# A two-layer convolution megakernel: conv 1's stores on ScalarE's queue, and another order of loads and work where the layers meet

## The chip, the cores and the metric

The program runs on one core of one Trainium2 chip. The metric is device time in microseconds of one execution, from which the median of several runs is taken. The engines are called PE (TensorE's matmuls), PEld (its weight loads), DVE (VectorE), ACT (ScalarE), POOL (GpSimd) and SP (SyncE, which only issues transfers here).

## What is computed

Two residual layers on x of 4 images, 64 channels, 256 x 256, all in float32.

```python
def layer0(v):                                   # v = group_norm(x)
    h = gelu(conv3x3(v, c1_w))
    xa, k = split(conv1x1(h, c2_w))
    xs = gelu(conv_vertical3(conv_horizontal3(xa)))         # depthwise
    mask = top2(softmax(mean(xs) @ gate_w.T))               # per image
    out = xs + sum(mask[i] * w3[i](w2[i](k) * w1[i](xs)) for i in range(3))
    return conv1x1(out, proj_w)

def layer1(v):                                   # v = group_norm(y)
    h = relu(batch_norm(conv3x3(v, quantize(w1)) + b1))     # statistics over all 4 images
    h = batch_norm(conv3x3(h, quantize(w2)) + b2)
    return relu(h + v)

y = x + layer0(group_norm(x))
result = y + layer1(group_norm(y))
```

A group norm needs the whole image before it can be applied, the mask needs an image's whole `xs`, and a batch norm needs all four images. These are what divide the work into passes.

## The kernel before

Tensors lie with 64 channels times two halves of the rows on the 128 partitions. An image is cut into 16 chunks of 8 rows a partition (`NCH`; 1 MB each) and, for layer 0's outputs, into 32 octets of half that size (`NOCT`). There are five stages.

1. **Front**: for each of 64 units (an image's chunk), layer 0's 3x3 convolution, the taps, the gelu and the low-rank terms. Results `xs` and the ranks go to DRAM (`xs_d`, `low_d`).
2. **Layer 0's outputs**: once an image's mask is known, its octets are made: `low_load`, `xs_load` and `out_load` (the residual x, tile `y`) bring the inputs, `out_slot` runs 16 matmuls (`out_open`, tile `ps_o`), adds them to `y` on DVE (`out_add`, L848), takes statistics, and after every second octet `out_store` (L861) sends `y` to `y_d`. Images 0, 1 and most of image 2 are done between the units of the front. The last 10 octets of image 2 and all 32 of image 3 are done between the chunks of stage 3 (`plan_out_late`).
3. **Conv 1** of layer 1: `conv1_load` brings normal rows of `y_d` (tile `yn`, L882), POOL takes row differences (L342), ACT normalises and copies them (L345, L358, L900), DVE makes the lower halves (L352 in `conv1_lower`, L361 in `conv1_lower_odd`), PE runs 12 matmuls on odd rows (`conv1_odd`, tile `ps_hm`) and two groups of 12 (`conv1_even`, tile `ps_h`) a chunk, ACT makes the shared term `m` (L311), DVE makes the result `h` in two halves (`conv1_out`, L317), ACT squares it for the statistics (`conv1_square`, L381), and a store sends it to `h1_d` (L956; the profile leaves numbers out and calls it `h_d`).
4. **Conv 2** over all 64 chunks, from `h1_d`.
5. **The end**: batch norm, residual sums and the store of the result.

**What sets the order.** Every engine works in its program's order. In stages 1 to 3 that order is written out by hand: `at(step, order, call)` puts a call in a table, and the calls are issued sorted by step and, in a step, by order. A unit of the front has two steps, so the front has 128; conv 1 begins at step `CONV1` = 128, and each chunk has four: chunk k of image b has its odd matmuls at T = 128 + 65 b + 4 k. `plan_conv1` puts a chunk's load at T - 13, its differences at T - 7, its result's two halves at T + 8/3 and T + 4, and its square at T + 16/3. For chunks 0 to 2 of image 0 the places are lists of their own. `TAIL` says where the last units' steps fall among conv 1's: `front_taps_h` (L683, L686), `front_taps_i` (L677), `front_k_out` (L733) and others. `divide` is a small POOL instruction (L485) that waits for the taps' matmuls.

All transfers are issued by SP, in the same order: an issue that waits (for a result, a free buffer, or the landing of an earlier transfer) holds up all issues behind it. Completion is told by eight semaphores taken in turn.

**Buffers that matter here.** `y` has two, of 1 MB (tag "o"); the late `xs_in` shares three (tag "h"); `ranks` has two. Conv 1's `h` has two in turn, chosen in `conv1_out`, but for image 0 the chunks 0, 1 and 2 all take the same one:

```python
if k % 2 and (b > 0 or k > 2):
    h_out[b, k] = flat(chunk_x(f"h1_{b}_{k}"))[:, 0 : CPAIR * W].rearrange("p (a b) -> p a b", b=W)
else:
    h_out[b, k] = conv1_pool[0].tile([P, CPAIR, W], F32, tag="h1", name=f"h1_{b}_{k}", bufs=1)
```

Of the kernel before, what the change touches and what calls it, by code (L numbers as in the profile page):

```python
# [27 lines left out]
NG = NPAIR // GP  # L28
NOCT = NG // 2
CG = 4  # L30
CPAIR = CG * GP
# [10 lines left out]
def conv_preact_kernel(ctx: ExitStack, tc: tile.TileContext, io, col128, colset, col64):  # L42
    nc = tc.nc
# [21 lines left out]
    h1_d = [dram.tile([P, NSKEW, W], F32, name=f"h1_d{b}") for b in range(B)]  # L65
    h2_d = [dram.tile([P, NPAIR, W], F32, name=f"h2_d{b}") for b in range(B)]

    def flat(t):
        return t.rearrange("p a b -> p (a b)")
# [23 lines left out]
    def chunk_x(name):  # L93
        return first_pool.tile([P, CPAIR, PW], F32, tag="x", name=name, bufs=1)
# [25 lines left out]
    def at(step, order, call, *args):  # L120
        plan[step, order].append((call, args))
# [9 lines left out]
    def c128(name):  # L131
        return m128[:, col128[name][0] : col128[name][1]]
# [152 lines left out]
    def group_norm(st, avg, out, name):  # L285
        mv = stat.tile([P, 1, 2], F32, tag="mv", name=f"mv_{name}")
        nc.vector.bn_aggr(mv[:, 0, :], flat(st))
        yield
        yield from combine(mv, 1, avg, eps, out, name)
# [89 lines left out]
    def square(name, h, junk, total, rows=slice(0, P)):  # L379
        n = h.shape[1] * W  # L380
        nc.scalar.activation(  # L381
            junk[rows, 0:n], flat(h), AF.Square, bias=less[name][rows], accum_out=total
        )
# [440 lines left out]
    def out_open(b, n):  # L824

        k, sub, i = n // 2, n % 2, n % 4
        if n == 0:
            st_y[b] = lstat.tile([P, NG, 6], F32, tag="st_y", name=f"st_y{b}")
        ps = open_o[b, n] = bank("p", f"ps_o_{b}_{n}")
        xs = xs_in[b, k][:, sub]  # L830
        low = lows[b, k // 2].rearrange("p s (r w) -> p s r w", w=W)
        rounds(
            *(
                [
                    ((ps[:, x], p, x, c128("proj"), xs[:, :, p, :], (0, 2)), dict(start=True, stop=False, skip_group_check=True)),
                    ((ps[:, x], p, x, wm[b][:, i, :], low[:, :, p, :], (0, 2)), dict(start=False, stop=True, skip_group_check=True)),
                ]
                for x in range(2)
                for p in range(2)
            )  # L840
        )
# [4 lines left out]
    def out_add(b, n):  # L846
        ps, y = open_o.pop((b, n)), out_rows(b, n)
        nc.vector.scalar_tensor_tensor(y, ps.rearrange("p x s w -> p x (s w)"), out_bias[b], y, ALU.add, ALU.add)  # L848

    def out_stats(b, n):  # L850
        y = out_rows(b, n)
        for i in range(2):
            nc.vector.bn_stats(st_y[b][:, 2 * n + i, :], y[:, i])
        if n % 2:
            k = n // 2
            del xs_in[b, k]
            if k % 2:
                del lows[b, k // 2]

    def out_store(b, k):  # L860
        nc.sync.dma_start(y_d[b][:, k * CPAIR : (k + 1) * CPAIR, :], ys.pop((b, k)))  # L861

    def out_slot(b, n):
        out_open(b, n)
        out_add(b, n)
        out_stats(b, n)
        if n % 2:
            out_store(b, n // 2)

    def out_end(b):  # L870
        gn2[b] = const.tile([P, 3], F32, name=f"gn2_{b}")
        yield from group_norm(st_y.pop(b), c128("avg4"), gn2[b][:, 0:2], f"y{b}")
        nc.vector.tensor_scalar(gn2[b][:, 2:3], gn2[b][:, 0:1], gn2[b][:, 1:2], -1.0, ALU.mult, ALU.mult)
# [64 lines left out]
    def conv1_out(b, k, g):  # L938
        if g == 0:
# [4 lines that stand above are left out]
        h = h_out[b, k]  # L944
        at_h = h[:, 4 * g : 4 * g + 4, :]
        first = k == g == 0
        total = sums[b][:, 2 * k + g : 2 * k + g + 1]
        leave(at_h, open_h.pop((b, k, g)), m_in[b, k][:, g], "w1", None if first else total)
        if first:
            nc.vector.tensor_reduce(total, h[:, 1:4, :], AX.XY, ALU.add)  # L950
            nc.vector.tensor_reduce(sums[b][0:C, NOCT : NOCT + 1], h[0:C, 0, :], AX.X, ALU.add)
            if b == 0:
                totals_less("h1", h[:, 1:3, :])
        if g:
            del m_in[b, k]
            nc.sync.dma_start(h1_d[b][:, k * CPAIR : (k + 1) * CPAIR, :], h)  # L956

    def conv1_square(b, k):
        h = h_out.pop((b, k))
        square("h1", h[:, 1:, :] if k == 0 else h, junks[0], squares[b][:, k : k + 1])  # L960
        if k == 0:
            square("h1", h[0:C, 0:1, :], junks[0], squares[b][0:C, NCH : NCH + 1], slice(0, C))

    def conv1_end(b):

# [48 lines left out]
    def at_each(places, chain):  # L1014

        for place in places:
            at(*place, next, chain, None)

    F_STEPS = NOCT
    CONV1 = B * F_STEPS  # L1020
# [2 lines left out]
    TAIL = {  # L1023
        (0, 1.15): (0, 1.15), (0, 1.55): (0, 1.55), (0, 4.7): (0, 4.7), (0, 2): (0, 2), (0, 2.2): (0, 2.2),
        (0, 4): (0, 13.2), (0, 4.15): (0, 13.3), (0, 5.2): (0, 13.4), (0, 5.3): (0, 13.5), (0, 8.6): (1, 13.9),
        (0, 9.2): (3, 13.35), (0, 7): (2, 13.2), (0, 7.2): (2, 13.25), (0, 8): (3, 13.1), (0, 9): (3, 13.2), (0, 9.1): (3, 13.3),
        (1, 1.15): (3, 13.4), (1, 1.55): (3, 13.5), (1, 4.7): (4, 13.9), (1, 2): (5, 13.2), (1, 2.2): (5, 13.25),
        (1, 4): (6, 13.2), (1, 4.15): (6, 13.3), (1, 5.2): (6, 13.4), (1, 5.3): (6, 13.5), (1, 8.6): (7, 13.9),
        (1, 8): (8, 13.2), (1, 8.1): (8, 13.3),
# [128 lines left out]
    def plan_out_late(b, ns, steps, order, end):  # L1158

        for n, step in zip(ns, steps):  # L1160
            if n % 2 == 0:
                at(step - 5, 0.2, low_load, b, n // 2)
                at(step - 5, 0.3, xs_load, b, n // 2, "h")
                at(step - 4, 0.4, out_load, b, n // 2)
            at(step, order, out_slot, b, n)
        at_each(end, out_end(b))

    def conv1_first():
# [12 lines left out]
    def plan_conv1(b):  # L1181
        t = CONV1 + b * (NG + 1)
        if b == 0:
            at(t - 4, -1, conv1_first)
            at(t, 12, conv1_open)
        for k in range(NCH):
            T = t + 4 * k
            places = [T + p for p in (-13, -7, -6, -5, -4, -4, -4, -3)]
            if b == 0 and k < 3:
                places = [t + p for p in ((-6, -3, -3, -2, -2, -2, -1, -1), (-4, -1, -1, 0, 0, 0, 0, 1), (-2, 1, 2, 3, 4, 4, 4, 5))[k]]  # L1190
            load, diff, odd, up0, up1, low_odd, low0, low1 = places

            def late(step, order):
                return (step, 5.5 + (order - 13) if step < t else order)

            at(load, 0, conv1_load, b, k)
            at(*late(diff, 13.08), conv1_differences, b, k)
            at(*late(odd, 13.1), conv1_upper_odd, b, k)
            at(*late(up0, 13.12), conv1_upper, b, k, 0)
            at(*late(up1, 13.14), conv1_upper, b, k, 1)  # L1200
            at(*late(low_odd, 13.2), conv1_lower_odd, b, k)
            at(*late(low0, 13.22), conv1_lower, b, k, 0)
            at(*late(low1, 13.24), conv1_lower, b, k, 1)
            at(T, 13, conv1_odd, b, k)
            at(T + 4 / 3, 13, conv1_even, b, k, 0)
            at(T + 4 / 3, 13.15, conv1_shared, b, k)
            at(T + 8 / 3, 13, conv1_even, b, k, 1)
            at(T + 8 / 3, 13.05, conv1_out, b, k, 0)
            at(T + 4, 13.05 if k < NCH - 1 else 12.9, conv1_out, b, k, 1)
            at(T + 4 + 4 / 3, 13.16, conv1_square, b, k)  # L1210
        at(t + NG, 12.95, conv1_end, b)
        at(t + NG + 1, 13.06, conv1_end_out, b)
        at(t + NG + 3, 13.3, conv1_close, b)

    plan_front()
    for b in range(B):
        if b < B - 1:
            plan_stats(b + 1)
            plan_out(b, NOCT if b < B - 2 else 22)
            if b == B - 2:  # L1220
                plan_out_late(b, range(22, NOCT), [CONV1 + 16 + 3 * n for n in range(10)], 13.6, [(CONV1 + n, 12.6) for n in (48, 50, 50, 52, 52, 52, 54)])
        else:
            t, e = CONV1 + 42, CONV1 + b * (NG + 1) - 10
            steps = [t + (e - 6 - t) * n // (NOCT - 1) for n in range(NOCT)]
            plan_out_late(b, range(NOCT), steps, 13.6, [(e - i, 15) for i in (5, 3, 3, 1, 1, 1, -1)])
        plan_conv1(b)
# [116 lines left out]
    with tc.manual_schedule(  # L1343
# [8 lines left out]
        n = len(chunks)  # L1352
# [62 lines left out]
    for i, (b, k) in enumerate(steps):  # L1415
        if i + AHEAD < len(steps):
            end_load(i + AHEAD)
        y, h = y_of.pop(i), h2.pop((b, k))
# [120 lines left out]
```

## Time and profile before

| | |
|---|---|
| median of 3 runs | 3040.98 us (3035.65 to 3042.23) |
| profiled execution | 3027.39 us, span of the program's instructions 3025.4 us |
| PE busy in the span | 2364.3 us (78%) |
| DVE busy | 2467.0 us (82%) |
| ACT busy | 2054.0 us (68%) |
| POOL busy | 1677.4 us (55%) |
| moved by DMA | 915.35 MB, mean 303 GB/s |
| mean granted clock of PE | 0.912 |

The page is one profiled execution. Its engine rows count an engine as busy while an instruction runs, not while it waits; a row of waits gives engine, line and what ended the wait, with microseconds in total, the number of times and the longest. "SPq" is SP's queue, so its rows tell what the issue of transfers stood waiting for. In the chain of waits a "DMA" piece reaches from a transfer's issue to its landing. Conv 1's first matmuls start at 1320 us, its last end at 2025; conv 2 runs from 2035 to 2585.

### The profile page before, as it was taken

How to read it: one execution, taken by the hardware profiler on the slowest of the kernel's cores; microseconds unless marked ns; L12 is line 12 of the kernel's file. 1: busy time of each engine (PE TensorE's matmuls, PEld its weight loads, DVE VectorE, ACT ScalarE, POOL GpSimd, SP SyncE). 2: the span in 40 equal slices, each digit the busy share in tenths (PEclk: the TensorE clock that was granted, in tenths of full speed). 3: DMA queues.
4: the chain of work that ended last, by engine and by line, in shares of the span. 5: the costliest groups of instructions: out<-in, count | busy, mean ns of one | idle time of the engine just before them, and what ended most of it. 6: DMA issues, size and time to landing. Idle time of an engine off the chain costs nothing.

```text
span 3025.4 us, 53036 instructions
## 1 busy us (share of the span) xinstructions
PE 2364.3 (78%) x21576; PEld 1504.4 (50%) x21576; DVE 2467.0 (82%) x2793; ACT 2054.0 (68%) x2274; POOL 1677.4 (55%) x1210
## 2 busy tenths in 40 slices
PE   1898899998999999978889999989999999100000
PEld 1444444444544445545556667767888888100000
DVE  5668688888888899968788888979998998876665
ACT  6798887786876555556566677878888888432222
POOL 5888887776877778834445455635555555000000
PEclk9999999999999999999999999999999999655555
DMA  8565479999999879849889898756777763899999
GB/s 344 188 238 224 185 263 371 350 349 346 342 341 329 301 280 328 291 157 322 315 327 332 336 339 321 262 207 238 257 273 262 266 243 138 333 425 424 424 425 410
DMA packets 135572, 915.35 MB, mean 303 GB/s; under 512 B 14944, under 2 KB 15712, under 8 KB 40608
## 3 DMA queue, kind: packets, MB, share of 16 engines
q1 hardware_dynamic: 135328, 911.97, 80.3%
q8 instruction: 169, 2.77, 0.4%
q14 instruction: 75, 0.61, 0.1%
HBM read 573.74 MB, written 338.17 MB: 301 GB/s over the span
## 4 chain that ended last, share of the span: by engine, by line
PE 28%; DMA 18%; DVE 5%; issue 2%; ACT 1%; SPq 1%; POOL 0%; DVEq 0%; ACTq 0%
PE ps_h L295 18%; PE ps_h2m L295 6%; DMA y_end<-y_d 5%; DMA h<-h_d 4%; DMA out<-h 4%; PE ps_hm L295 3%; DMA y<-in_xp 3%; DMA xs_in<-xs_d 2%; PE ps_o L492 2%; DVE h L317 1%; DVE diff L352 1%; DVE y L848 1%; DVE odd L361 1%; DMA y_d<-y 1%; SPq L822 0%
## 5 line engine op out<-in xcount | busy, mean ns | idle before, releaser
L295 PE MATMUL ps_h<-diff,w_q 128*128 128x512 f32 x3072 | 751.3, 399 | 9.1 <-DVE h L317 9.1
L295 PEld LDWEIGHTS ps_h<-diff,w_q 128*128 128x128 f32 x3072 | 577.1, 189 | 180.9 <-issue 25.8
L492 PE MATMUL ps_c<-v,us 64*64 64x256 f32 x9216 | 547.2, 386 | 41.4 <-DVE ps_c L623 35.6
L342 POOL TENSOR_TENSOR d<-yn 128x1024 f32<-128x1024 f32 x128 | 355.0, 2793 | 313.7 <-DMA yn<-y_d 179.8
L492 PEld LDWEIGHTS ps_c<-v,us 64*64 64x64 f32 x9216 | 363.6, 136 | 199.8 <-DVE ps_c L623 44.9
L342 POOL TENSOR_TENSOR d<-h 128x1024 f32<-128x1024 f32 x127 | 311.9, 2477 | 194.8 <-DVE diff L350 130.0
L492 PE MATMUL ps_a<-h,av 64*64 64x512 f32 x4080 | 387.9, 493 | 38.8 <-DVE t L686 28.7
L317 DVE SCALAR_TENSOR_TENSOR h<-ps_h,scale_w,m 128x1024 f32<-128x1024 f32 x256 | 323.6, 1279 | 64.2 <-PE ps_h L295 48.1
L540 POOL TENSOR_TENSOR x<-x 128x512 f32<-128x512 f32 x256 | 330.3, 1290 | 12.5
L1420 ACT ACTIVATE v<-y_end,shift,gn 128x2048 f32<-128x2048 f32 x64 | 133.8, 2093 | 279.7 <-DMA y_end<-y_d 244.5
L492 PEld LDWEIGHTS ps_a<-h,av 64*64 64x64 f32 x4080 | 153.9, 134 | 307.5 <-issue 204.3
L381 ACT ACTIVATE junk<-h,less_h 128x2048 bf16<-128x2048 f32 (+3 forms) x133 | 255.9, 1924 | 11.1 <-DVE h L317 10.9
L848 DVE SCALAR_TENSOR_TENSOR y<-ps_o,ob,y 128x1024 f32<-128x1024 f32 x128 | 163.9, 1280 | 118.9 <-DMA y<-in_xp 62.9
L1421 DVE SCALAR_TENSOR_TENSOR h<-h,ss,v 128x2048 f32<-128x2048 f32 x64 | 149.8, 2350 | 120.8 <-ACT v L1420 80.3
L683 DVE SCALAR_TENSOR_TENSOR t<-ps_a,m,t 128x1020 f32<-128x1020 f32 x128 | 163.3, 1276 | 104.1 <-ACT t L677 102.7
L677 ACT ACTIVATE t<-ps_a,tap_bias,m 128x1024 f32<-128x1024 f32 x128 | 154.1, 1204 | 97.8 <-PE ps_a L492 97.3
L705 ACT ACTIVATE xs<-t 128x1024 f32<-128x1024 f32 x128 | 134.9, 1054 | 121.2 <-DVE t L689 92.6
L295 PE MATMUL ps_h2m<-odd,w_q 128*128 128x512 f32 x768 | 193.2, 400 | 8.2 <-DVE odd L361 4.4
L295 PE MATMUL ps_hm<-odd,w_q 128*128 128x512 f32 x768 | 193.0, 400 | 4.2 <-ACT k L733 2.4
L352 DVE SCALAR_TENSOR_TENSOR diff<-d,gn,diff 128x1024 fp32r<-128x1024 f32 x128 | 188.1, 1499 | 4.7 <-ACT diff L345 4.7
L345 ACT ACTIVATE diff<-d 128x1024 fp32r<-128x1024 f32 x128 | 135.1, 1055 | 83.4 <-POOL d L342 82.1
L532 POOL TENSOR_TENSOR x<-x,x 128x512 f32<-128x512 f32 x128 | 161.0, 1279 | 43.3 <-ACT x L526 43.3
(226 smaller groups left out, 4321.8 us busy)
## 6 DMA issues: line engine op xcount, KB each, us to landing
h_d<-h SPq DMA_DIRECT2D x114, 1024.0 KB
x<-in_xc SPq DMA_DIRECT2D x64, 1280.0 KB
h<-h_d SPq DMA_DIRECT2D x64, 1152.0 KB
yn<-y_d SPq DMA_DIRECT2D x60, 1152.0 KB
xs_in<-in_xp SPq DMA_DIRECT2D x64, 1024.0 KB
xs_d<-xs SPq DMA_DIRECT2D x128, 512.0 KB
xs_in<-xs_d SPq DMA_DIRECT2D x64, 1024.0 KB
y<-in_xp SPq DMA_DIRECT2D x64, 1024.0 KB
```

The costliest lines, as they stand in the source:

```text
L295: nc.tensor.matmul(ps, wq[w][:, kind, kx, :], t[:, rows, kx : kx + W], start=(j == 0), stop=(j == len(terms) - 1))
L317: nc.vector.scalar_tensor_tensor(h.rearrange("p (e k) w -> p e (k w)", e=2), ps.rearrange("p e k w -> p e (k w)"), w_scale[w], m.unsqueeze ...
L342: engine.tensor_tensor(raw.rearrange("p (g r) w -> p g r w", g=2), *pair, ALU.subtract)
L352: nc.vector.scalar_tensor_tensor(lower, raw, scale, upper.bitcast(F32), ALU.mult, ALU.subtract)
L381: nc.scalar.activation(junk[rows, 0:n], flat(h), AF.Square, bias=less[name][rows], accum_out=total)
L492: last[:] = [nc.tensor.matmul(ps[o, at_out[0] : at_out[1], :], w[i], rhs[i], **flags)]
L532: nc.gpsimd.tensor_tensor(x4[:, j - 1], x_rows(u, j + 2), x4[:, j - 1], ALU.subtract)
L540: nc.gpsimd.tensor_tensor(x[:, r : r + 2], x[:, r + 2 : r + 4], x[:, r : r + 2], ALU.subtract)
L677: nc.scalar.activation(flat(t), flat(ps), AF.Identity, bias=tap_bias, scale=sh[:, 1:2])
L683: nc.vector.scalar_tensor_tensor(t[:, :, 1:W], ps[:, :, 0 : W - 1], sh[:, 0:1], t[:, :, 1:W], ALU.mult, ALU.add)
L848: nc.vector.scalar_tensor_tensor(y, ps.rearrange("p x s w -> p x (s w)"), out_bias[b], y, ALU.add, ALU.add)
L1421: nc.vector.scalar_tensor_tensor(h, h, ss2[:, 0:1], v, ALU.mult, ALU.add)
```

## The change

- The store of conv 1's result moves from `conv1_out` (SP, after the second half of `h`) to `conv1_square` (ACT's queue, after the square).
- `out_store` leaves `out_slot`; `plan_out_late` puts it one step later, at order 13.3.
- In `plan_out_late` the loads of `ranks` and `xs_in` move from 5 to 9 steps ahead of the octet, and the load of `y` from 4 to 6.
- Image 2's last ten octets are 4 steps apart (3 before), image 3's 32 start at `CONV1` + 56 (+ 42 before) and still end at the same step; image 2's statistics close 8 steps later.
- Where the layers meet: `front_k_out` of the last units goes ahead of `front_taps_i` on ACT; for image 0's chunk 0 the lower differences move behind `front_taps_h`, and its odd matmuls ahead of the last units' taps; chunk 3's `conv1_upper_odd` goes later within its step.

```diff
@@ out_slot
         out_open(b, n)
         out_add(b, n)
         out_stats(b, n)
-        if n % 2:
-            out_store(b, n // 2)
@@ conv1_out
         if g:
             del m_in[b, k]
-            nc.sync.dma_start(h1_d[b][:, k * CPAIR : (k + 1) * CPAIR, :], h)
@@ conv1_square
         if k == 0:
             square("h1", h[0:C, 0:1, :], junks[0], squares[b][0:C, NCH : NCH + 1], slice(0, C))
+        nc.scalar.dma_start(h1_d[b][:, k * CPAIR : (k + 1) * CPAIR, :], h)
@@ TAIL
-        (0, 9.2): (3, 13.35), (0, 7): (2, 13.2), (0, 7.2): (2, 13.25), (0, 8): (3, 13.1), (0, 9): (3, 13.2), (0, 9.1): (3, 13.3),
+        (0, 9.2): (3, 13.25), (0, 7): (2, 13.2), (0, 7.2): (2, 13.25), (0, 8): (3, 13.1), (0, 9): (3, 13.2), (0, 9.1): (3, 13.3),
@@ plan_out_late
             if n % 2 == 0:
-                at(step - 5, 0.2, low_load, b, n // 2)
-                at(step - 5, 0.3, xs_load, b, n // 2, "h")
-                at(step - 4, 0.4, out_load, b, n // 2)
+                at(step - 9, 0.2, low_load, b, n // 2)
+                at(step - 9, 0.3, xs_load, b, n // 2, "h")
+                at(step - 6, 0.4, out_load, b, n // 2)
             at(step, order, out_slot, b, n)
+            if n % 2:
+                at(step + 1, 13.3, out_store, b, n // 2)
@@ plan_conv1
+            first = b == k == 0
+
             def late(step, order):
                 return (step, 5.5 + (order - 13) if step < t else order)

             at(load, 0, conv1_load, b, k)
             at(*late(diff, 13.08), conv1_differences, b, k)
-            at(*late(odd, 13.1), conv1_upper_odd, b, k)
+            at(*late(odd, 13.36 if b == 0 and k == 3 else 13.1), conv1_upper_odd, b, k)
             at(*late(up0, 13.12), conv1_upper, b, k, 0)
             at(*late(up1, 13.14), conv1_upper, b, k, 1)
             at(*late(low_odd, 13.2), conv1_lower_odd, b, k)
-            at(*late(low0, 13.22), conv1_lower, b, k, 0)
-            at(*late(low1, 13.24), conv1_lower, b, k, 1)
-            at(T, 13, conv1_odd, b, k)
+            at(*((t, 1.3) if first else late(low0, 13.22)), conv1_lower, b, k, 0)
+            at(*((t, 1.32) if first else late(low1, 13.24)), conv1_lower, b, k, 1)
+            at(T, 1.9 if first else 13, conv1_odd, b, k)
@@ the plan of images 2 and 3
             if b == B - 2:
-                plan_out_late(b, range(22, NOCT), [CONV1 + 16 + 3 * n for n in range(10)], 13.6, [(CONV1 + n, 12.6) for n in (48, 50, 50, 52, 52, 52, 54)])
+                plan_out_late(b, range(22, NOCT), [CONV1 + 16 + 4 * n for n in range(10)], 13.6, [(CONV1 + n, 12.6) for n in (56, 58, 58, 60, 60, 60, 62)])
         else:
-            t, e = CONV1 + 42, CONV1 + b * (NG + 1) - 10
+            t, e = CONV1 + 56, CONV1 + b * (NG + 1) - 10
             steps = [t + (e - 6 - t) * n // (NOCT - 1) for n in range(NOCT)]
```

## The prediction

> **What bounds the kernel now.** I read the page first (PE busy 78% of the span, no engine full), then the busy times by stage, which say where time can be had at all.
>
> ```profile
> core 0: us, PE busy (x) PEld busy (x) DVE busy (x) ACT busy (x) POOL busy (x), PEclk, DMA share, GB/s
> ...
> 1280.00:1376.00 96.00, 77.55 (x649) 45.33 (x652) 67.69 (x78) 59.81 (x65) 41.36 (x27) 0.96 0.51 196
> 1376.00:1862.00 486.00, 446.60 (x2158) 300.32 (x2151) 407.87 (x464) 316.33 (x304) 230.20 (x85) 0.97 0.89 329
> 1862.00:2025.00 163.00, 161.54 (x695) 129.46 (x693) 147.56 (x155) 136.22 (x134) 93.66 (x36) 1.00 0.71 261
> ...
> 2585.00:3025.00 440.00, 1.13 (x5) 0.80 (x4) 298.76 (x151) 135.41 (x68) 0.00 (x0) 0.51 0.99 415
> ```
>
> The change touches three of these. In the hand-over (1280 to 1376) PE idles 18.5 us of 96. In the mixed stage (1376 to 1862: conv 1 with layer 0's last 42 outputs between its chunks) it idles 39.4 of 486. In the rest of conv 1 (to 2025) it is full. Conv 2 is full on PE and the last stage is full on DMA; neither is touched. So at most some 58 us of idle time is in reach. Who ends it in the mixed stage, for PE, DVE and SP's queue in turn:
>
> ```profile
> PE ps_o L492 <- DMA xs_in<-xs_d: 21.6, 9, 6.2
> PE ps_h L295 <- DVE h L317: 8.0, 5, 2.2
> PE ps_h_end L295 <- DVE h L317: 4.3, 2, 2.7
> PE ps_o L492 <- DVE y L848: 3.8, 1, 3.8
> ```
> ```profile
> DVE y L848 <- DMA y<-in_xp: 37.9, 8, 9.0
> ```
> ```profile
> SPq L956 <- DVE h L317: 240.2, 39, 16.3
> SPq L861 <- DVE y L848: 101.4, 21, 9.1
> SPq L803 <- DMA y_d<-y: 42.9, 4, 15.6
> ```
>
> The reader is to see one story in three views. PE waits 21.6 us for the `xs_in` loads themselves, and 17.8 us for DVE (the three rows and 1.7 us for a small chain), which in its turn stood 37.9 us at L848 for `y`. Both loads are late because SP, which issues every transfer in order, stands at L956 (the store of conv 1's result, `h_d` here) and at L861 for 342 of 486 us. The chain of waits shows how long a transfer then takes, from issue to landing, in microseconds:
>
> ```profile
> 1420.05 16.44 DMA xs_in<-xs_d
> ...
> 1451.44 15.97 DMA y_d<-y
> ...
> 1467.46 4.90 DMA y<-in_xp
> ```
>
> 16 us for 1 MB is queueing, not bandwidth: alone, right after a pause, 4.9 us were enough. One step of the plan lasts 486/163 = 3.0 us here (42 outputs over steps 144 to 307), so the leads of 5 steps (xs) and 4 steps (y) are 15 and 12 us, plus what is left of the step: just what a landing takes, so every second one is late.
>
> **What the Trainium skill says.** "DMA: Bandwidth & Descriptors", section "Queues, rings and completion order": SP and ACT each own a row of rings on the same 16 DMA engines, and each engine takes packets from its rows in turn. So a store from ACT needn't stand behind SP's backlog; the trace of before has one row only and can't show it. Same page, "Issuing engines are not separate DMA queues": a second issuing queue adds no bandwidth. I follow that. "SBUF — State Buffer", section "Who interferes with whom", says that a DVE operation with two SBUF inputs and a GpSimd operation that reads SBUF shut each other out; the trace agrees: `odd` (L361) takes 1.2 us alone and 3.5 us under a GpSimd operation from 1910 on. "TensorE: Matmul & The Clock Gate", Part 1: the array's clock falls after idling; here the 16 matmuls of `ps_o` after the 6.2 us gap at 1430 take 3.7 us, against 1.9 without a gap.
>
> **Part 1, the stores move to ACT.** SP loses 64 issues and, what counts, the 240 us at L956. ACT gains 64 issues. SP's issue takes 0.32 us (L956, median, 0.38 at most); the longest of its conv 1 loads took 1.47. No ACT issue is in the trace: 0.32 to 1.5 us each; a gain is excluded, as an instruction is added. I take 0.4: 16 us in the mixed stage, where ACT idles 170, and 0.4 for each 8.44 us chunk later, where ACT idles 27 us over some 19 chunks (1.4 each). Cost 0 to 2 us; I take 1. Queued behind it on ACT are the next chunk's L900, L358 and L345; the wait for `h` is already over, since the square just ahead needed it. One more wait is possible: transfers here use eight semaphores in turn, and an issue waits until the eighth before it has landed (SP's L812 waits so for `ranks`, which it doesn't read: 41.1 us over the span). If ACT's take part in that turn, it may stand a little. Eight transfers are about 8 steps, 22 us, and landings end at 20: 0 to 5 us, I take 0.
>
> The store now leaves after the square, 3.3 to 4.7 us later than at present. Its buffer is wanted again two chunks on. In the trace the square of a chunk ends 9 to 27 us before the leave that reuses the buffer (mixed) and 8 to 10 us before it (after 1870), where such stores land in 3.8 to 6.4 us (here and below, from the issue to the last update of its semaphore ahead of the next use). Hidden, with 2 us to spare. But chunks 0 to 2 of image 0 share one buffer:
>
> ```profile
> 1353.45 1.28 DVE L317 SCALAR_TENSOR_TENSOR h<-ps_h,scale_w,m 128x1024 f32<-128x1024 f32 x1
> ...
> 1364.59 1.28 DVE L317 SCALAR_TENSOR_TENSOR h<-ps_h,scale_w,m 128x1024 f32<-128x1024 f32 x1 [4.13 <-ACT junk L381]
> ```
>
> Chunk 2's first leave starts right when chunk 1's square ends; its store had been gone since 1354.8. Now the store is issued only there, and PE (whose next bank this leave frees) waits for it to land: 0.4 + 3.8 to 6.2 us (landings from 1285 to 1380), 4 to 9 with loads beside it. I take **+5.5**. Between chunks 0 and 1 there are 6.6 us from square to leave: nothing.
>
> **Part 2, order in the hand-over.** PE's timeline:
>
> ```profile
> 1315.74 4.38 PE L492 MATMUL ps_a<-h,av 64*64 64x512 f32 x24 [7.56 <-DVE t L686]
> ...
> 1338.04 3.07 PE L295 MATMUL ps_hm<-odd,w_q 128*128 128x512 f32 x12 [2.36 <-ACT k L733]
> ```
>
> In the 7.56 us DVE did conv 1's two lower differences (4.2 us, from 1308.85) ahead of L683/L686, which had their input from ACT at 1309.8. Moved behind them, `t` is ready at 1312.4, 3.2 us sooner; and conv 1's first 12 matmuls (3.0 us, their input ready at 1304.5) go into the gap. GpSimd's in-order tick and the next image rows follow `ps_a`, so the gain is passed on: 6.2 less some 1.2 lost where ACT's differences stay ahead. `k` (L733) ahead of the tap copy: 1.7 of the 2.36. L900/L358 of chunk 3 behind the tap copy: 0.8 of the next gap's 1.7. Sum **-7.5**. With part 1 the hand-over gives **-2**.
>
> **Part 3, sooner and even loads.** xs leads by 9 steps, 25 us; landings reach 22 at most (16.4 typical when thick): 19.6 of 21.6 us go. y leads by 6 steps and is no longer behind L956. It has two buffers of 8 steps; it can't be issued before the store 5 steps ahead (14 us) has landed, which took 5 to 16. So y comes at about 6 steps, 16 us and 4 more for the output's own place in the step, against landings of 13 typical and 19 at most: I take 10 of the 17.8 us off, for DVE works in order and a late y delays the leaves behind it. The output store moves to the next step, so that SP meets it when DVE is done. The even spacing (4 steps for 3, then 4.4) does nothing by itself: the same 42 outputs in the same 163 steps; it ends the 42.9 us of waits at L803. Slow matmuls after gaps: 41 chunks at 8.43 and 42 outputs at 1.9 us make 425, PE shows 446.6; a quarter of that excess, 5 us, goes with the gaps. Against it, DVE (408 us busy, blocked by GpSimd at times) gets closer to PE: +3. Stage: -19.6 - 10 - 5 + 3 = **-31.6**, to 454.
>
> **Sum**: -2 - 31.6 + 1 = **-32.6 us** on the profiled execution (span 3025.4 in 3027.39): 2995. The median shown is 3040.98, 13.6 above that execution; the same difference puts the forecast at **3008**. Its own range is 2994 (all idle time in the mixed stage and the hand-over's 7.5 gone) to 3020.
>
> **Rivals.** (a) *The transfers are the bound.* 329 GB/s for 486 us is 160 MB; the stage's thick stretches (share 0.95) move 344 GB/s: 465 us, -21, with the rest -22: **3019**. For it: the share of 0.89. Against: 415 GB/s in the last stage. (b) *SP finds the next thing to stand at*: L861, L803 or the turn of eight semaphores take up what L956 leaves, and loads are no sooner; only -2 and +1 remain: **3040**, no change. (c) *Slower: the stores from ACT come too late for the two buffers.* A buffer's cycle is two leaves 2.5, to the square's end 4, issue 0.4, landing L: 7 + L, and has two chunks, 23.7 us now (486/41). It decides from L = 16.7 us on. y's stores landed in 15 to 18 where transfers were thick; if all of conv 1's take 18, a chunk takes 12.6 us, 41 of them 517, +31, and the hand-over pays 9 for 5.5: about **3076**. Against it: the ring of its own, and a median of 9.0 us for these stores in the mixed stage.
>
> **Chances.** Forecast 0.58, (a) 0.22, (b) 0.09, (c) 0.11. A measurement here tells 0.2% (6 us) from no change: faster 0.80, same 0.09, slower 0.11. The range from 2990 to 3034 takes in the forecast's and (a)'s bounds and leaves out (b), (c) and a little at the low end.
>
> **What would show it.** Right: PE's wait for `xs_in` below 4 us, DVE's for `y` below 15, the mixed stage near 454 us; the 7.56 us gap gone; a new wait of 4 to 9 us of DVE for a landing of `h_d` at chunk 2. (a): mixed stage near 465 with DMA share over 0.95. (b): SP's waits renamed, not shorter. (c): waits of L317 for `h_d<-h` in most chunks. It would be wrong if DVE, not PE, ended most waits of the new mixed stage.

## The result, and the profile after

The changed kernel takes **3017.11 us** (median of 6 runs, 3012.65 to 3023.50), beside 3039.82 for the kernel before in the same comparison (3033.64 to 3042.23): ratio 0.9933 with a 95% interval from 0.9918 to 0.9948, so 16 to 25 us are gained. The forecast was 3008 with a range from 2990 to 3034. Its sign was right and the time lies in the range; two terms of its sum were wrong. The profiled execution took 3016.92 us, span 3015.1.

First the busy times by stage of the kernel after, in the columns of the prediction's first view:

```profile
1280.00:1376.00 96.00, 73.15 (x600) 42.90 (x593) 59.48 (x67) 54.30 (x59) 38.17 (x24) 0.89 0.52 184
1376.00:1850.00 474.00, 452.36 (x2208) 307.99 (x2206) 430.43 (x475) 323.35 (x311) 232.53 (x86) 0.99 0.91 340
1850.00:2014.00 164.00, 157.51 (x676) 126.53 (x676) 144.79 (x161) 136.95 (x137) 93.57 (x39) 1.00 0.68 257
```

In the mixed stage PE idles 21.6 us of 474 (39.4 of 486 before). In the hand-over it idles 22.9 of 96 (18.5 before): worse, in spite of the new order. Now the waits of PE, DVE and SP's queue from 1376 to 1850:

```profile
PE ps_h L295 <- DVE h L317: 5.6, 5, 2.7
PE ps_h_end L295 <- DVE h L317: 4.8, 1, 4.8
PE ps_o L492 <- DMA xs_in<-xs_d: 3.8, 1, 3.8
```
```profile
DVE y L848 <- PE ps_h L295: 23.0, 4, 8.2
DVE y L848 <- PE ps_o L492: 7.4, 9, 1.5
DVE y L848 <- issue: 6.5, 1, 6.5
```
```profile
SPq L861 <- DVE y L848: 194.9, 21, 22.6
SPq L803 <- DMA y_d<-y: 139.5, 19, 13.1
SPq L880 <- DMA xs_in<-xs_d: 17.2, 5, 4.3
SPq L861 <- DMA ranks<-low_d: 15.2, 4, 4.3
SPq L861 <- DMA yn<-y_d: 12.0, 4, 3.8
```

PE's wait for `xs_in` fell from 21.6 to 3.8 us. Its waits for DVE did not fall: all its rows for DVE, of which the first two are shown, add up to 17.5 us (17.8 before). DVE's first and third rows name PE and "issue", but what DVE lacked was `y`. Its instruction and the load of that tile, from the timelines of DVE and SP:

```profile
1580.13 1.28 DVE L848 SCALAR_TENSOR_TENSOR y<-ps_o,ob,y 128x1024 f32<-128x1024 f32 x1 [6.47 <-issue]
```
```profile
1558.45 0.33 SPq L803 DMA_DIRECT2D y<-in_xp  x1
```

By the semaphores, the store of `y` issued at 1546.59 landed at 1558.38. The load into its buffer left at 1558.45, landed at 1580.05, and DVE began at 1580.13. The four waits of the first row end in the same way, within 0.1 us of landings of `y` at 1624.37, 1666.56, 1763.98 and 1810.64. So DVE waited 29.5 us for `y`, in five places. Counted in the same way it was 44.9 before: the 37.9 that its row names, and 7.0 that another row puts down to PE. And SP stands no less than before: L956 is gone, but L861 for DVE has grown by 93.5 us, L803 by 96.6, and the last three rows bring 44.4, which make 234 of L956's 240.

The page shows the second queue, with packets, MB and share of time:

```profile
q1 hardware_dynamic: 126112, 844.85, 75.0%
q10 hardware_dynamic: 9216, 67.11, 5.5%
```

67.11 MB are the 64 stores. To compare versions I read anchors from PE's timeline: the end of the front's last `ps_c` matmul, and the first odd matmul (`ps_hm`) of chunks 2, 4 and 46. Times in us of one profiled execution each:

| version | front's end to chunk 2 | chunk 2 to 4 | chunk 4 to 46 | front's end to 46 | chunk 46 to 63 |
|---|---|---|---|---|---|
| before | 48.1 | 21.1 | 497.9 | 567.1 | 144.9 |
| after | 40.8 | 36.6 | 474.1 | 551.6 | 144.8 |
| after, chunk 1's own buffer | 40.8 | 19.6 | 482.4 | 542.8 | 144.9 |
| after, stores back on SP | 44.0 | 21.1 | 472.4 | 537.4 | 144.9 |

From the front's end to chunk 46 the change gains 15.6 us. The rest of the execution, which the change doesn't touch, took 2313 us before and 2319 in the other three, and from 2310 to 2320 in all the executions of this document, so medians of runs decide on totals, and the anchors only tell where.

### The profile page after: what moved, and what is told of

The parts are those of the page before. It is cut to its first block, busy times and chain, and to the rows that moved or that the text cites. A ratio compares the mean times of both kernels' runs of the same rounds, so it can differ in the third digit from the quotient of the medians.

```text
span 3015.1 us, 52987 instructions
## 1 busy us (share of the span) xinstructions
PE 2357.4 (78%) x21576; PEld 1503.4 (50%) x21576; DVE 2478.0 (82%) x2793; ACT 2054.8 (68%) x2274; POOL 1676.3 (56%) x1210
## 3 DMA queue, kind: packets, MB, share of 16 engines
q10 hardware_dynamic: 9216, 67.11, 5.5%
## 4 chain that ended last, share of the span: by engine, by line
PE 28%; DMA 18%; DVE 5%; issue 2%; ACT 1%; POOL 0%; SPq 0%; DVEq 0%; ACTq 0%; POOLq 0%
PE ps_h L295 18%; PE ps_h2m L295 6%; DMA y_end<-y_d 5%; DMA h<-h_d 4%; DMA out<-h 4%; PE ps_hm L295 3%; DMA y<-in_xp 2%; DVE diff L352 1%; PE ps_o L492 1%; DMA y_d<-y 1%; DVE h L317 1%; DMA h_d<-h 1%; DMA yn<-y_d 1%; DMA xs_in<-xs_d 1%; DVE odd L361 1%
## 5 line engine op out<-in xcount | busy, mean ns | idle before, releaser
L295 PE MATMUL ps_h<-diff,w_q 128*128 128x512 f32 x3072 | 753.8, 400 | 14.3 <-DVE h L317 13.7
L317 DVE SCALAR_TENSOR_TENSOR h<-ps_h,scale_w,m 128x1024 f32<-128x1024 f32 x256 | 322.8, 1279 | 76.6 <-PE ps_h L295 53.9
L381 ACT ACTIVATE junk<-h,less_h 128x2048 bf16<-128x2048 f32 (+3 forms) x133 | 256.0, 1925 | 11.1 <-DVE h L317 11.0
L848 DVE SCALAR_TENSOR_TENSOR y<-ps_o,ob,y 128x1024 f32<-128x1024 f32 x128 | 163.7, 1279 | 80.6 <-DMA y<-in_xp 27.4
L352 DVE SCALAR_TENSOR_TENSOR diff<-d,gn,diff 128x1024 fp32r<-128x1024 f32 x128 | 208.5, 1658 | 0.3 <-ACT diff L345 0.3
```

Of the source, the lines that this page charges most:

```text
L295: nc.tensor.matmul(ps, wq[w][:, kind, kx, :], t[:, rows, kx : kx + W], start=(j == 0), stop=(j == len(terms) - 1))
L317: nc.vector.scalar_tensor_tensor(h.rearrange("p (e k) w -> p e (k w)", e=2), ps.rearrange("p e k w -> p e (k w)"), w_scale[w], m.unsqueeze ...
L352: nc.vector.scalar_tensor_tensor(lower, raw, scale, upper.bitcast(F32), ALU.mult, ALU.subtract)
L381: nc.scalar.activation(junk[rows, 0:n], flat(h), AF.Square, bias=less[name][rows], accum_out=total)
```

## The experiments

Each was timed against the kernel before, on the chip on which it ran itself (medians of before from 3035 to 3040 us). "Gain" is 3040 us times one less the ratio, so that all stand on one scale.

| version | median | ratio, 95% interval | gain |
|---|---|---|---|
| the whole change | 3017.11 | 0.9933 [0.9918, 0.9948] | 20 |
| part 1 alone (stores from ACT) | 3027.70 | 0.9968 [0.9955, 0.9980] | 10 |
| part 2 alone (order) | 3030.87 | 0.9978 [0.9968, 0.9988] | 7 |
| part 3 alone (loads) | 3005.54 | 0.9898 [0.9878, 0.9918] | 31 |
| parts 2 and 3 | 2999.01 | 0.9868 [0.9852, 0.9884] | 40 |
| whole, chunk 1's own buffer | 3008.54 | 0.9904 [0.9889, 0.9919] | 29 |
| the same, and SP made to stop | 3016.45 | 0.9924 [0.9909, 0.9938] | 23 |
| the same, stores late on SP | 3008.01 | 0.9901 [0.9879, 0.9922] | 30 |
| the same, stores at the old place on SP | 3000.85 | 0.9879 [0.9858, 0.9899] | 37 |
| whole, ACT's stores for chunks 4 to 45 only | 3003.94 | 0.9893 [0.9874, 0.9913] | 33 |
| xs's lead alone | 3030.69 | 0.9977 [0.9964, 0.9989] | 7 |
| even spacing alone | 3025.90 | 0.9961 [0.9948, 0.9975] | 12 |
| xs's lead and even spacing | 3010.89 | 0.9914 [0.9891, 0.9936] | 26 |

### Chunk 1 in a buffer of its own

```diff
-            if k % 2 and (b > 0 or k > 2):
+            if k % 2:
```

> The changed kernel, but image 0's chunk 1 of conv 1 takes the second result buffer, so that chunks 0, 1 and 2 no longer share one. Theory (the shared buffer makes chunk 2's first result wait for the landing of chunk 1's store, which now leaves late and into a burst of loads): the PE gaps of 6.05 and 6.42 us near 1355 and 1365 go, the odd matmuls of chunk 4 start near 1366 instead of 1380, and the time falls by 10 to 14 us, to about 3005. Rival (the burst of loads and the wait for the ranks' store hold the hand-over up in any case): the gaps move by a few microseconds, and the time falls by less than 4 us.

Measured: 3008.54 us, 9 us (0.0029) better than the whole change and a little less than the 10 to 14 that were expected. The two places in PE's timeline, after and then with the buffer:

```profile
1361.12 4.40 PE L295 MATMUL ps_hm<-odd,w_q 128*128 128x512 f32 x12 [6.05 <-ACT m L311]
1371.94 8.48 PE L295 MATMUL ps_h<-diff,w_q 128*128 128x512 f32 x24 [6.42 <-DVE h L317]
```
```profile
1357.76 3.08 PE L295 MATMUL ps_hm<-odd,w_q 128*128 128x512 f32 x12 [0.16 <-ACT m L311]
1360.68 5.78 PE L295 MATMUL ps_h<-diff,w_q 128*128 128x512 f32 x24
```

Both gaps are gone, and the matmuls behind them are no longer slowed. Chunks 2 to 4 take 17.0 us less; 8.3 of that are given back by chunk 46. So the shared buffer is a real cost of the store's new place.

### Each part alone, and the whole without part 1

Three edits put one part of the diff into the kernel before: the first its `conv1_out` and `conv1_square` hunks (part 1), the second its `out_slot` and `plan_out_late` hunks and the spacing (part 3), the third its `TAIL` and `plan_conv1` hunks (part 2). The fourth takes part 1 out of the kernel after.

> The kernel before with part 1 alone: conv 1's stores from ACT's queue, all else as before. Theory (the leads of the loads are what counts, the store's place only helps them): the hand-over loses 5 to 12 us, the mixed stage wins 5 to 12 us, 3035 to 3045 in all. Rival (SP's 240 us of standing at the store was the cause of the late loads): the mixed stage wins 20 us or more, 3020 to 3027.

> The kernel before with part 3 alone: sooner and even loads and the output store a step later, conv 1's stores still on SP. Theory (the leads are what counts): PE's wait for xs_in falls below 5 us, no loss in the hand-over, the time falls by 18 to 28 us to 3012 to 3022, at least as far as with the whole change. Rival (loads stay late behind the stores on SP): less than 8 us, 3032 or more.

> The kernel before with part 2 alone: the order of work where the layers meet. Theory: 6 to 9 us less at conv 1's chunk 2 and all of it kept, 3031 to 3034. Rival (what is won before chunk 3 is waited for again, as conv 1's inputs or the ranks' store come no sooner): within 3 us of before.

> The changed kernel with conv 1's stores back on SP after the result's second half: parts 2 and 3 without part 1. Theory (the stores on ACT's queue cost some 12 us in the hand-over and a few more among the last outputs): 2998 to 3004 where before is 3037, that is 13 us or more below the whole change; no wait of 6 us on PE between 1350 and 1375. Rival (part 1 costs only what chunk 1's buffer explains, so the order in part 2 is what is lost): 3004 to 3010.

Measured, in gains: 10 for part 1, 31 for part 3, 7 for part 2, and 40 for parts 2 and 3 together. Parts 1 and 3 did better than their theories (part 1 all but reached its rival's 3020 to 3027); the other two came as expected. Parts 2 and 3 add up (38 of their own, 40 together). **Part 1 does not: alone it gains 10, on top of the other two it loses 20.** The version without it has the lowest median of all, 2999.01 us, and beats both kernels.

With part 1 alone, chunks 4 to 46 took 482.7 us (497.9 before) and chunks 2 to 4 took 29.5 (21.1 before). What it buys is `xs_in`, through SP's freedom: PE's wait for it fell from 21.6 to 10.0 us, in this one row of its waits from 1376 to 1850.

```profile
PE ps_o L492 <- DMA xs_in<-xs_d: 10.0, 2, 8.6
```

Part 3 buys more with SP still standing at the store. With part 3 alone, chunks 4 to 46 took 474.0 us, as with the whole change (474.1). PE has no wait for `xs_in`, and only two waits of DVE, 5.5 us, end with a landing of `y`, while SP's waits in that stretch read:

```profile
SPq L954 <- DVE h L317: 165.5, 37, 11.2
SPq L861 <- DVE y L848: 107.7, 20, 8.6
SPq L803 <- DMA y_d<-y: 96.4, 16, 11.6
```

L954 is the store. Loads of `xs_in` that are placed 9 steps ahead came in time here in spite of stops of up to 11 us in their queue; at 5 steps they didn't. That is why the two remedies don't add: once the leads are long and the spacing even, the relief of SP has nothing left to buy, and only its price stays.

Part 2 alone gained 5.7 us up to chunk 4 in its profile and lost 6.4 from there to chunk 46; its median gained 7 all the same.

### Is the rest SP's running ahead?

Against the stores on SP, the version with the extra buffer still lacked some 10 us. I suspected that SP, without its stop at the store, issues `yn` and `xs_in` ahead of the `y` that is wanted first. The edit keeps the extra buffer and gives the stop back: a store of one column of chunk k's sums, to a new tensor `stop_d`, from SP at the old place (64 transfers of 512 bytes more).

```diff
         if g:
             del m_in[b, k]
+            nc.sync.dma_start(stop_d[:, NCH * b + k : NCH * b + k + 1], total)
```

> The changed kernel with chunk 1's own buffer, and on SP, where the store of conv 1's result used to stand, a store of one column of 4 bytes a partition that waits for the same result: SP stops again where it stopped before, while the 1 MB store stays on ACT's queue. It adds 64 small transfers. Theory (SP, no longer held, queues image rows and xs ahead of y, so y lands late): waits of DVE at the output sum fall from 30 us to below 15, 3000 to 3004. Rival (the stores on ACT's ring take their share at once and slow the loads): DVE's waits stay, 3008 or more.

Measured: 3016.45 us, slower by 0.0020, in intervals that overlap. DVE's waits for `y` stayed (30.6 us, counted by the landings; 26.2 without the stop). So the suspicion was not borne out, but this is no clean refutation either. The added transfers take part in the turn of eight semaphores: SP stood 48.6 us at L862 for landings of `ranks` and 27.1 at L881 for landings of `y`, neither of which those transfers need. The stop was bought with another wait.

### Lead and spacing apart

```diff
-                at(step - 5, 0.2, low_load, b, n // 2)
-                at(step - 5, 0.3, xs_load, b, n // 2, "h")
+                at(step - 9, 0.2, low_load, b, n // 2)
+                at(step - 9, 0.3, xs_load, b, n // 2, "h")
```

> The kernel before with only the loads of ranks and xs at 9 steps ahead, spacing, y's lead and all else as before. Theory (PE's 21.6 us of waits for xs are a loss of their own): 12 to 18 us less, 3019 to 3025. Rival (xs only hides y, which then ends the waits): less than 8 us.

The spacing alone is the diff's last hunk. The third version has both.

> The kernel before with only the even spacing of the last 42 outputs (4 steps apart from step 144 on, image 3 from step 184). Theory (as predicted, spacing alone does nothing): within 4 us of before. Rival (the first ten outputs, 3 steps apart, are where most of the waits stand): 10 us or more below before.

> The kernel before with layer 0's last outputs evenly spaced and the loads of ranks and xs 9 steps ahead; y stays at 4 steps and the store of y in its old place. Spacing alone gave 10.8 us, the leads of ranks and xs alone 6.0, all of the load part 31.2. Theory (the parts help each other: even spacing thins the queue and the lead then lets xs arrive): more than the sum, 3008 to 3014. Rival (they only add, and the rest comes from y's lead and the later store): 3020.

Measured: 7, 12 and 26. The first two came as their rivals, not their theories, had it. With the lead alone PE no longer waits for `xs_in`, but DVE still does for `y` (the second row, too, ends with landings of `y`), and PE now waits 15.9 us for DVE at L848, where it was 3.8:

```profile
DVE y L848 <- DMA y<-in_xp: 25.3, 4, 9.7
DVE y L848 <- issue: 14.4, 2, 9.5
```

So one late load had hidden the other. With the spacing alone it is the reverse: DVE's wait for landings of `y` falls from 37.9 to 5.0 us, and PE still waits for `xs_in`:

```profile
PE ps_o L492 <- DMA xs_in<-xs_d: 19.6, 7, 4.3
```

Together they gain 26. That this is more than the sum of 7 and 12 was expected, but the difference is within the intervals. Chunks 4 to 46 took 475.0 us with both, 496.0 and 491.3 with either, 497.9 before. `y`'s longer lead and the later store add at most 5 to reach part 3's 31, which the intervals don't tell from nothing.

### Row or place?

Three versions to split the price of part 1. The first issues the stores where the change does, but from SP; the second has them at their old place on SP; both have the extra buffer.

```diff
-        nc.scalar.dma_start(h1_d[b][:, k * CPAIR : (k + 1) * CPAIR, :], h)
+        nc.sync.dma_start(h1_d[b][:, k * CPAIR : (k + 1) * CPAIR, :], h)
```

> The whole change with chunk 1's own buffer, and every store of conv 1's result issued behind the square, as in the change, but from SP's queue. So SP meets a store only when its result has long been made and doesn't stop there: it runs ahead as in the change, but all transfers share one row of rings. With ACT's queue this version took 3008.5 us, with the stores on SP at their old place (chunk 1 sharing its buffer) 2999.0. Theory 1 (the second row is the cause: ACT's stores overtake the loads that stand in SP's row): about 2999, and no SP wait for h. Theory 2 (SP's run-ahead is the cause: without the stop at h it issues rows and xs ahead of the y that is wanted first): about 3008.5, with SP standing at L861 and L803 for over 250 us in the mixed stage, and DVE's waits for y at 25 us or more.

> Control: orders and loads as in the change, stores on SP at their old place (2999.0 us), and chunk 1 of image 0 in a buffer of its own. With ACT's stores that buffer gave 8.5 us. Theory (it gives only because ACT's store leaves into a burst): here chunk 2's first leave waits for the square of chunk 1, a few us at most, so 2997 to 2999. Rival (the shared buffer costs much wherever the store is): 2991 to 2993.

> The whole change, with ACT issuing the stores of chunks 4 to 45 only (those beside layer 0's last outputs), and SP those of chunks 0 to 3 and of 46 to 63 at their old place; no buffer added. Theory (the loss against stores on SP has two separate places, 8.5 us at chunk 1's buffer and 9.5 us in the mixed stage, and none in the quiet stage or in conv 2): 3008.5, with hm2 to hm4 back at 21 us and the mixed stage as in the version with its own buffer. Rival (the mixed stage's part is a consequence of the hand-over's, a debt of late chunks): 2999 to 3002.

Measured: 3008.01, 3000.85 and 3003.94.

The second version, the control, came within 2 us of its theory: where the stores stay on SP at their old place the extra buffer shows no gain (0.9879, beside 0.9868 without it, in overlapping intervals). The 9 us belong to the store from ACT and the shared buffer together.

The first has the time that theory 2 named, and the 260 us at L861 and L803, but not DVE's waits for `y`: no wait of DVE ends with a landing of `y`. The premise failed, too, for SP still stood at the store 33 times (L960). What DVE waited for was the landing of its own result's store, because the buffer of two chunks before was not free (4.6 us in the control). SP's rows and this one of DVE:

```profile
SPq L861 <- DVE y L848: 165.3, 21, 15.3
SPq L960 <- DVE h L317: 110.5, 33, 7.6
SPq L803 <- DMA y_d<-y: 94.7, 16, 11.2
```
```profile
DVE h L317 <- DMA h_d<-h: 13.1, 7, 3.4
```

So this run shows neither the row nor the running ahead to be the cause. It shows something simpler: at the same late place in the order, ACT's row has no advantage in time over SP's (0.9904 and 0.9901), though the stores land in 10.1 us from ACT and in 15.5 from SP (medians over chunks 14 to 43). The sooner stores took away DVE's 13.1 us of waits for `h_d`, but there DVE waited 26.2 us for `y`, against none.

The third falls between its two expectations. With chunks 0 to 3 back on SP, 12 us of the 20 come back (0.9893; its interval lies wholly under that of the whole change), and chunks 2 to 4 take 21.1 us again. So most of part 1's price is paid in the hand-over, none of it from chunk 46 on. What is left for the mixed stage is about 6 us, from 0.9893 to the mean of 0.9868 and 0.9879, and the intervals overlap. By the anchors it is 0.6 or 6.1: from the front's end to chunk 46 this version took 538.0 us, the two with all stores on SP 537.4 and 531.9. **Whether it is there at all, and its cause, stay open.** The traces offer one candidate, later landings of `y` (median 16.0 us and 28.0 at most in the kernel after, 13.6 and 21.2 with the stores on SP), but no run isolates it. Open, too, is why the extra buffer's gain was in part given back: chunks 4 to 46 took 482.4 us there and 481.9 with the stores late on SP, but 474.2 in this third version.

## Why the prediction was right or wrong, step by step

| step of the forecast | forecast | measured |
|---|---|---|
| order in the hand-over | -7.5 | -7.3 to chunk 2 (after), -5.7 to chunk 4 (part 2 alone) |
| ACT's store at chunk 1's buffer | +5.5 | +15.5 from chunk 2 to 4; 9 to 12 in the medians; +8.4 with part 1 alone |
| ACT's issue in full chunks | +1 | -0.1 from chunk 46 to 63 |
| PE's wait for xs | -19.6 | -17.8 |
| PE's waits for DVE, through y | -10 | -0.3 |
| the mixed stage in all | -31.6 | -23.8 from chunk 4 to 46 |
| even spacing by itself | 0 | -6.6 from chunk 4 to 46, -12 in the median (alone) |

In sum, -32.6 us was forecast up to chunk 46, and the anchors show -15.6. That the time still lies in the range is due to its width: it was made to take in rival (a) as well. The forecast had named a sign of being wrong, that DVE should end most waits of the new mixed stage. It does: 17.5 of the 21.3 us of PE's waits.

**The xs term** was right as a wait. As time it was not 19.6 us: the lead alone took the whole wait away and gained 7. Its reason was only half right, too: it counted on SP being free of L956, and part 3 alone shows that the lead and the spacing suffice.

**The hand-over term, +5.5 us, was mis-sized by 10.** The forecast saw the right wait at the right instruction, L317 of chunk 2. It took the issue to come 0.4 us after the square and the landing from the traces of before, 3.8 to 6.2 us, with 9 as its upper bound. Here is what happened, from DVE, ACT and SP of the kernel after:

```profile
1347.84 1.28 DVE L317 SCALAR_TENSOR_TENSOR h<-ps_h,scale_w,m 128x1024 f32<-128x1024 f32 x1 [3.56 <-DMA h_d<-h]
...
1370.60 1.28 DVE L317 SCALAR_TENSOR_TENSOR h<-ps_h,scale_w,m 128x1024 f32<-128x1024 f32 x1 [11.62 <-DMA h_d<-h]
```
```profile
1359.87 1.21 ACT L311 ACTIVATE m<-ps_hm,m,scale_w 128x1024 f32<-128x1024 f32 x1 [12.33 <-DMA low_d<-k]
1359.94 0.33 ACTq L960 DMA_DIRECT2D h_d<-h  x1
1360.97 1.99 ACT L381 ACTIVATE junk<-h,less_h 128x2048 bf16<-128x2048 f32 x1
```
```profile
1356.85 0.32 SPq L747 DMA_DIRECT2D low_d<-k  x1
1357.26 0.38 SPq L803 DMA_DIRECT2D y<-in_xp  x1
1357.69 1.31 SPq L880 DMA_DIRECT2D yn<-y_d  x2
1359.06 1.10 SPq L822 DMA_DIRECT2D ranks<-low_d  x2
```

Chunk 1's `h` was ready at 1350.3. Its store stood in ACT's order behind chunk 2's `m` (L311), which waited until 1359.87 for the landing of `low_d`, a store of the front's last unit that SP could issue only at 1356.85. (ACT waits so in the kernel before, too, 5.8 us at 1361.37; but there the store did not stand behind it.) Right behind it SP let go all that had stood behind it: `y`, two `yn`, two `ranks`, then `xs_in` and another `y`. The store left 9.6 us after its data and into this burst, and landed 10.5 us later, when DVE began at 1370.60. In the kernel before, the same store left at once and landed in 3.8. Chunk 0's store did the same in small (issued 4.0 us late, 8.8 to land, against 0.0 and 4.2): the 3.56 us of DVE at 1347.84, where the forecast said "nothing". The delay feeds itself: what follows DVE's first late `h`, `k` (L746) and so `low_d`, came 6.5 us later after the front's end than with the extra buffer, where ACT's wait is back at 5.84:

```profile
1356.50 1.21 ACT L311 ACTIVATE m<-ps_hm,m,scale_w 128x1024 f32<-128x1024 f32 x1 [5.84 <-DMA low_d<-k]
```

With part 1 alone chunk 1's first `h` met no such wait, and the stretch from chunk 2 to 4 grew by 8.4 us, within the forecast's 4 to 9. In the whole change that `h` could start 7.8 us sooner after the front's end, and chunk 0's store landed in 8.8 us, against 4.9 with part 1 alone; so the two met. No run tells the new order and the sooner loads apart here. So the wait was named rightly, and its price was about right in the old plan. The forecast added the parts as if they didn't touch, and it never asked what ACT itself waits for there.

**The y term, -10 us, failed altogether.** The forecast took 10 of PE's 17.8 us of waits for DVE as waits for `y` that would end once `y` was no longer behind L956. Two steps of this did not hold. The first is that `y` then comes in time. `y` has two buffers, and its cycle is a chain: DVE's add, the store's issue, its landing, the issue of the load into the same buffer, its landing, the next add. Means of 19 cycles, in us:

| version | add to store's issue | store's landing | to the load's issue | load's landing | sum |
|---|---|---|---|---|---|
| before | 0.3 | 10.8 | 8.1 | 12.8 | 31.9 |
| after | 0.0 | 11.4 | 0.1 | 17.0 | 28.6 |
| after, stores back on SP | 0.2 | 11.5 | 0.4 | 15.1 | 27.2 |

In the kernel before, the load left 8.1 us after it could; the change freed it of that. But 4.3 us of it went into the load's longer landing. With the stores on SP, where SP stood at L954 for 167.8 us, the load left just as soon, so the lead and the spacing, not the relief of L956, freed `y`. DVE's waits for `y` were 44.9, 29.5 and 5.8 us in these three (the forecast named below 15 as its sign).

The second step is that PE's waits for DVE come through `y`. With the stores on SP they added up to 20.2 us, more than the 17.8 of before, though `y` was hardly ever late. Most of them are for L317, and DVE was busy for 448 of the 474 us.

Rival (b) came true in part: SP found the next thing to stand at. It was not true that nothing remains then: `xs_in`, placed ahead of those stops, came in time.

**The spacing** was called idle by itself. 42 outputs over the same steps bring the same transfers, but before, the first ten came every third step. All the 42.9 us that SP stood at L803 fall in this stretch, and PE idled 18.0 us in it, 12.6 of them for `xs_in`. With the spacing alone PE idled 3.6 us there. Chunks 4 to 13 took 127.5 us before and 97.8 with the spacing alone. A part of that is work put off (ten octets in that stretch in place of thirteen), but the median gained 12 us.

**Rivals.** (a), transfers as the bound, gave 3019 and lies nearest to the result, but not for its reason: the mixed stage moved 340 GB/s at a DMA share of 0.91 (its sign was over 0.95), and the version with the stores on SP is 18 us faster at 345 GB/s and 0.92. (c) did not come: no wait of L317 for `h_d` appears in the mixed stage of the kernel after; it came for chunks 1 and 2 only, where the buffer is shared, and in small (13.1 us) where the late stores went from SP. Its sum has a slip: 7 + 18 us for two chunks are 12.5 a chunk, not 12.6, and with its own terms it comes to some 3070.

**The Trainium skill's places.** "DMA: Bandwidth & Descriptors", section "Queues, rings and completion order", says that each DMA engine takes packets from its rows in turn. The traces fit, though they don't show the turns themselves: with the same loads, a store lands in 10.2 us from ACT and in 14.3 from SP (medians over chunks 14 to 43), and SP's landings of `y` take 17.0 us in place of 15.1 (means). "Issuing engines are not separate DMA queues" says that a second issuer saves the issue time alone; 340 GB/s with it and 345 without agree that it brought no bandwidth.

## What to carry to other kernels

A store that was moved to another engine's queue also waited for what that engine's earlier instruction waited for (9.6 us here); before such a move, ask of each store what stands ahead of it there, and which buffer is freed by its landing. Two remedies for the same late load need not add: here the longer leads and even spacing made the relief of SP's queue worthless, and only its price was left. Two changes where stages meet need not add either: part 1 cost 8.4 us there by itself and 15.5 on top of the other two. When a load is late, follow its buffer's whole cycle (last reader, store, landing, load), and ask whether the engine that waits for it is what the bounding engine waits for.

## What the runs showed of the hardware that was not expected

- **A DMA issue on ACT's queue overtook the arithmetic just ahead of it.** The store stands behind the square (L381) in the program, yet it was issued at 1359.94, 1.03 us before the square began and 0.07 after the start of the instruction before that. So it was for 59 of the 64 stores of the kernel after. It did not overtake that instruction (L311) while it waited for `low_d`. In the mixed stage ACT's stores left 0.2 us after `h` was made (median). "Perfetto Trace Analysis", section "DVE / Act Engine Instruction (TENSOR_ADD, Activation, etc)", fits: the sequencer pushes an instruction into a wait queue and goes on to the next. An issue on ACT took 0.33 us and cost nothing in the full chunks (144.8 us from chunk 46 to 63, 144.9 before).
- **The turn of eight semaphores runs over both queues.** In the kernel after, each of the eight tells of landings of both queues' transfers (from ACT 3 to 21 a semaphore). SP stands for landings of transfers that the waiting one doesn't need (L880 for `xs_in`, L861 for `ranks` and `yn`: 44.4 us), and so it does more in the version with 64 small transfers added. With parts 2 and 3 alone, all stores on SP, such rows are all but gone from the same stretch (0.5 us for `xs_in`, 0.2 for `h_d`).
